# One projected map tile for two, the residual's copy in quarters, and a planner with two shared transfer queues

## The chip, the cores and the metric

The kernel runs on one core of one Trainium2 chip. Its time is the device time of one execution in microseconds (us); a kernel's figure is the median of several. A profiled execution gives the span from the first to the last instruction, and what each engine did in it. The engines are TensorE (PE in the profile, its weight loads PEld), VectorE (DVE), ScalarE (ACT), GpSimd (POOL) and SyncE (SP), which here only starts transfers.

## What is computed

Eight images of 256 channels and 32 x 32 pixels go through two layers.

```python
# layer 0: convolutional attention (8 heads of 32 channels)
q = einsum('bchw,oc->bohw', gn(x), q_w)
kv = einsum('bchw,oc->bohw', gn(x), kv_w)        # 256 key and 256 value channels
def pooled(t):                                    # four levels: 32, 16, 11 and 5 a side
    # average-pool each level, add its 3x3 depthwise convolution, join: 1,426 keys
ks, vs = layernorm(pooled(k_map)), layernorm(pooled(v_map))
attn = softmax(q k^T * scale);  out = attn v      # then a mix from a global token, projection
x = x + out
# layer 1: on tokens (1,024 an image)
t = t + attention(ln(t))                          # one head of 256
t = t + sum_e w[:, e] * (relu(bn(relu(bn(ln(t) W1[e])) W2[e])) Wo[e])   # 8 experts
```

## The kernel before

The program is written as one long order for each engine. `Flow` records every instruction (so nearly all have line 670, that of its `call`), and while the program is built it keeps an account: when each engine would be free, when each tile would be ready or read, what an operation costs (`cost`), and after an operation's end a lag until its result can be used (`note`). Work outside the main loop is written as generators ("threads") with a rank; a thread says what it needs next, and `step` resumes those that `runnable` lets go: filler for PE is let in while a credit lasts or while the account says that PE would stand otherwise. `finish` resumes threads until a condition holds, without regard to the credit. So the costs and lags of the account decide where every piece of filler is put in each engine's order; at run time the order is fixed and the engines wait for one another through semaphores.

The main loop of `attention` has 360 steps, 45 for each image b. The queries of one half of the heads (c) and one half of the pixels make a unit of 11 key chunks; the last, short chunk of all four units is done at once, as one more step of the first unit (`tail_scores`, the joint last keys). A step is: four score matmuls into `sc` (four PSUM banks, one buffer), the exponential by ACT into one of six `pt` tiles, and the value matmuls of the step before into `pv`. For the sums, every odd `pt` is added into the even one by an accumulating transfer started by POOL, and VectorE adds the pairs (`sums`).

Beside these steps run, as threads: `prepare(b)` for the next image (load into `xi`, group statistics, pooling, then `maps`), `convolve` (the taps of the depthwise convolution on VectorE, `taps`), `value_tokens` and `key_tokens` (transposes and layer norm, which make `vt` and `kn`), `queries` and `fetch_queries`, `project`, and layer 1 (`layer1`, `outputs`, `norm`). What of layer 1 is not done by the loop's end runs beside the first part of `experts`, until the gates, which need all images, are there; until then the second expert layer is done plainly and put by in DRAM (`ahead`), after that both layers use seven products of quarter size.

The names that the change touches:
- `pmaps`, tags `p0` and `p1` of 128 x 1,426 floats: a projected map, of which there are four for an image (two of values, two of keys). `maps` writes it by ACT in three slices (columns 0, 512 and 1,024 on) beside the scaled `acc`; `taps` reads it: level 0 (eight taps over the first 1,024 columns), then the three small levels. `todo` counts maps begun, `read[0]` those whose level 0 was read, `done` those finished, `freed[0]` the pairs of `acc` set free. In `maps` the next map is begun when

```python
lambda: read[0] >= len(todo) - 1 and len(todo) < (3 + 2 * max(freed[0], 2) if freed[0] else 5)
```

  and its third slice when `len(done) >= len(todo) - 1`.
- `first_maps` makes image 0's maps, with two borrowed `pt` tiles and the two of `pmaps` to hold them.
- the residual: x[b] is copied to `t1[b]` in DRAM by SP when `prepare(b)` begins, and `project(b)` adds to it with transfers started by POOL (`t<-xr`). In the profile the copy is `t<-in_x_dram`, 1,024 KB, seven times; the last image has none. `layer1` loads `t1[b]` later.
- the lag of a transfer in `note`: 2.0 us and 0.0045 us a KB for SP, 1.5 us and 0.0078 us a KB for POOL, whatever else is on its way.

Of the kernel before, what the change touches and what calls it, by code (L numbers as in the profile page):

```python
# [16 lines left out]
P = 128  # L17
C = 256
HW = 1024
# [637 lines left out]
class Flow:  # L657
# [27 lines left out]
    def __init__(self, tc, kit):  # L685
        nc = tc.nc
        self.tc, self.kit = tc, kit
        self.now = dict.fromkeys(("PE", "DVE", "ACT", "POOL", "SP"), 0.0)
        self.last = {}
        self.ready, self.read, self.writer, self.reader, self.slots, self.open = {}, {}, {}, {}, {}, set()  # L690
        self.pe = self.Engine(self, "PE", nc.tensor)
        self.ve = self.Engine(self, "DVE", nc.vector)
        self.act = self.Engine(self, "ACT", nc.scalar)
        self.pool = self.Engine(self, "POOL", nc.gpsimd)
        self.sp = self.Engine(self, "SP", nc.sync)
        self.threads = []
        self.cut = {}
        self.also = {}
        self.tiled = None
        self.columns = False  # L700
        self.credit, self.port = [0.0, 0.0], 0.0

    def tile(self, pool, shape, tag, bufs=1):
# [60 lines left out]
    def note(self, engine, op, ins, args, kwargs):  # L764
        aps = [a for a in (*args, *kwargs.values()) if hasattr(a, "tensor") or hasattr(a, "space")]
        out = kwargs.get("out", args[0] if args else aps[0])
        srcs = [a for a in aps if a is not out]
        prev = self.last.get(engine)
        if prev is not None:
            self.tc.add_manual_dep(  # L770
                ins.ins,
                prev,
                mybir.DependencyInfo(mybir.DependencyClass.NoSync, mybir.DependencyReason.DATA),
                reason="program order",
            )
        self.last[engine] = ins.ins.name
        start = self.now[engine]
        names = [n for a in srcs for n in self.keys(a)]
        outs = self.keys(out)
        for n in (*names, *outs):  # L780
            if self.writer.get(n) != engine:
                start = max(start, self.ready.get(n, 0.0))
        for o in outs:
            if self.reader.get(o, engine) != engine:
                start = max(start, self.read.get(o, 0.0))
        cost = self.cost(engine, op, out, srcs)
        if engine == "PE":

            tiling = None if op == "transpose" else self.tiling(srcs)
            if tiling != self.tiled:  # L790
                cost += {None: 0.2, "rows": 0.2, "columns": 0.13, "both": 0.2}[tiling]
                self.tiled = tiling

        wide = [a for a in srcs if a.space != PSUM and a.free_size() > 4]
        if "dma" not in op and engine == "POOL" or engine == "DVE" and wide and (len(wide) > 1 or op in ("tensor_scalar", "tensor_copy")):
            start = max(start, self.port)
            self.port = start + cost
        self.now[engine] = end = start + cost
        lag = 0.15
        if "dma" in op:  # L800
            size = 4e-3 * out.shape[0] * out.free_size() if out.space != DRAM else 4e-3 * srcs[0].shape[0] * srcs[0].free_size()
            lag = 2.0 + 0.0045 * size if engine == "SP" else 1.5 + 0.0078 * size
        for n in {*outs, self.key(out)}:
            self.ready[n] = max(self.ready.get(n, 0.0), end + lag)
            self.writer[n] = "DMA" if "dma" in op else engine
        self.open.difference_update(names)
        for n in {*names, *map(self.key, srcs)}:
            self.read[n] = max(self.read.get(n, 0.0), end + lag)
            self.reader[n] = engine

    @staticmethod
    def key(a):
# [85 lines left out]
def attention(tc, kit, f, outer, ended, nb, consts, x, t1, t2, hn, bounds, vecs, q_t, kv_t, proj_t, gqk_t, wqk, wqkv, vecs1, w1_d, w1c, gate_d, wrc, vecs2, bnvec):  # L898
# [6 lines left out]
    with ExitStack() as ctx:  # L905
# [165 lines left out]
            f.pool.memset(t, 0.0)  # L1071
        made = [0]
        turn = [-1]
        todo, done, read, freed, key_parts, normalised = [], [], [2], [0], [0], [0]

        def pe(*tiles, tag=None):
            return "PE", tiles, tag
# [20 lines left out]
        def maps(xp):  # L1098

            for m in (2, 3, 0, 1):  # L1100
                c = m % 2
                yield until(
                    lambda: read[0] >= len(todo) - 1 and len(todo) < (3 + 2 * max(freed[0], 2) if freed[0] else 5)
                )
                p = pmaps[len(todo) % 2]
                acc = T(work, [P, NK], "acc", bufs=3)
                for s0, w in KEY_SLICES:
                    if s0 >= HW:
                        yield until(lambda: len(done) >= len(todo) - 1)
                    src = source(xp, s0, w)  # L1110
                    yield pe(src, tag="sm")
                    ps = small()
                    for k in range(2):
                        f.pe.matmul(
                            ps[:, :w],
                            lhsT=kvw[:, k, m * P : (m + 1) * P],
                            rhs=src[:, k, :],
                            start=k == 0,
                            stop=k == 1,
                        )  # L1120
                    f.act.activation(p[:, s0 : s0 + w], ps[:, :w], AF.Copy)
                    for s, n in enumerate(SIDES):
                        a, z = max(OFFS[s], s0), min(OFFS[s] + n * n, s0 + w)
                        if a < z:
                            f.act.activation(
                                acc[:, a:z],
                                ps[:, a - s0 : z - s0],
                                AF.Identity,
                                bias=db(c, s),
                                scale=mid[:, c * 4 + s : c * 4 + s + 1],  # L1130
                            )
                todo.append((c, p, acc))
# [4 lines left out]
            return dy, dx, max(0, -dy), n - max(0, dy), max(0, -dx), n - max(0, dx)  # L1137


        pmaps = [T(work, [P, NK], f"p{i}") for i in range(2)]  # L1140
        for t in pmaps:
            f.split(t, 512, HW)
        first, large, whole, pooled, asked = {}, [], [], [], []

        def first_diagonals():
# [11 lines left out]
        def first_maps(xp):  # L1157


            for m in range(4):  # L1160
                if m < 2:
                    p = T(work, [P, 4, 512], "pt", bufs=6).rearrange("p j q -> p (j q)")
                    acc = T(l1, [P, NK], "v") if m else T(work, [P, NK], "kn", bufs=3)
                else:
                    p = pmaps[m - 2]
                    acc = T(work, [P, NK], "acc", bufs=3)
                for t in (p, acc):
                    if t is not p or m < 2:
                        f.split(t, 512, HW)
                first[m] = p, acc  # L1170
            for m, s0 in [(m, s0) for g in (0, 2) for s0 in (0, 512) for m in (g, g + 1)] + [(m, HW) for m in range(4)]:
# [70 lines left out]
        def first_taps():  # L1242
            for m in (2, 3):
                yield until(lambda: "maps" in large)
                yield from taps(m - 2, 0, *first[m])
                large.append(("values", m))
                read[0] += 1
            yield until(lambda: whole)
            for m in (2, 3, 0, 1):
                for s in range(1, 4):  # L1250
                    yield from taps(m % 2, s, *first[m])
                whole.append(m)
            done.extend(first[m][1] for m in (2, 3, 0, 1))
# [109 lines left out]
        def prepare(b):  # L1363
# [1 line left out]
            if b:  # L1365
                yield until(lambda: len(asked) == 4)
            xi = xs.pop(b) if b in xs else load_x(b)
            if b < nb - 1:
                f.sp.dma_start(t1[b], x[b].rearrange("(k p) n -> p k n", p=P))
            st = T(work, [P, 2, 2, 6], "st")  # L1370
            mv = T(work, [P, 2, 2], "mv")
            for k in range(2):
# [518 lines left out]
        for i in range(len(steps) + 1):  # L1891
            if i < len(steps):
                b, c, half, kc = steps[i]
                sl = slice(half * 512, half * 512 + 512)
                if kc % 4 == 0:
                    f.finish(lambda: key_parts[0] > 3 * b + kc // 4)
                if (half, kc) == (0, 0):
                    f.finish(lambda: (b, c) in qs and (b or (c, 0) in asked))
                    turn[0] = 2 * b + c
                    atts[b, c] = T(work, [P, HW], "att", bufs=2)  # L1900
                if i == 4:
                    f.finish(lambda: {0, 1}.issubset(whole))
                if b == 0 and kc == 0:
                    f.finish(lambda: (c, half) in asked)
                if kc == NKC - 1:
                    f.finish(lambda: key_parts[0] > 3 * b + 2 and (b, 1) in qs and (b or len(asked) == 4))
                    tail_scores(b)
                else:
                    pts[i] = scores(b, c, sl, kc)
                f.step()  # L1910
# [709 lines left out]
```

## Time and profile before

| | us |
|---|---|
| median of 3 runs | 3294.26 (3291.0 to 3302.8) |
| the profiled execution | 3300.42 |
| its span | 3298.6 |
| first and last exponential of the main loop | 82.7, 1877.7 |

Mean granted TensorE clock: 0.978. Transfers moved 388 MB, a mean of 118 GB/s: 179.85 MB in the queue that POOL starts (28.1% of 16 engines' span) and 202.59 MB in that of SP (18.0%).

A row of busy times gives for each engine the us in which it was busy, the share of the span, and the instructions. In the rows of stretches the columns are: from and to, length, then busy us (and instructions) of PE, PEld, DVE, ACT, POOL, then the clock, the share of the 16 DMA engines, and GB/s. A row of waits reads: who waited for whom, us in total, times, longest. A row of the timeline: start, us, engine, line, operation, out<-in, shapes, count, and in brackets the idle time of that engine just before and what ended it. Buffer numbers are left out of names, so `p` is a map here and also a probability tile of layer 1, and `t<-in_x_dram` is `t1[b]`.

### The profile page before, as it was taken

What the parts mean: (1) busy time and instruction counts of PE and PEld (TensorE: products, weight loads), DVE (VectorE), ACT (ScalarE), POOL (GpSimd) and SP (SyncE); (2) the same over time, 40 slices, a digit from 0 to 9 for tenths busy, and PEclk for the clock granted to TensorE, in tenths of its full rate; (3) what the DMA queues carried; (4) which work ended last, traced back from release to release, by engine and by line L of the source; (5) the groups of instructions that cost most, each with busy time, mean ns of one, the idle gap of its engine ahead of it and who ended that gap; (6) DMA issues with size and microseconds to landing.
All of it is one profiled execution on the core that took longest, in us unless ns stands there. A gap on an engine that the chain in (4) does not pass through costs nothing.

```text
span 3298.6 us, 55657 instructions
## 1 busy us (share of the span) xinstructions
PE 3093.2 (94%) x22264; PEld 1793.6 (54%) x22264; DVE 2466.9 (75%) x4060; ACT 1692.0 (51%) x2298; POOL 1174.7 (36%) x1269
## 2 busy tenths in 40 slices
PE   8787899989989979999999989999999999999998
PEld 4322234324334323343433447776888888888887
DVE  5787898888887878979754544444888888887776
ACT  4466667656666657566656423334333333344443
POOL 2212314122141141232121120002856555577776
PEclk9799999989999999999999999999999999999999
DMA  2358666665575565656576662214444344300000
GB/s 75 78 117 183 135 149 126 129 153 105 125 172 104 135 152 95 152 122 123 126 165 122 144 229 74 77 63 161 141 141 142 139 163 163 122 20 33 20 13 21
DMA packets 118524, 388.06 MB, mean 118 GB/s; under 512 B 14560, under 2 KB 40488, under 8 KB 95024
## 3 DMA queue, kind: packets, MB, share of 16 engines
q0 software_dynamic: 28608, 179.85, 28.1%
q1 hardware_dynamic: 86288, 202.59, 18.0%
q8 instruction: 177, 2.90, 0.4%
q10 hardware_dynamic: 3360, 1.97, 0.2%
q14 instruction: 91, 0.75, 0.1%
HBM read 125.03 MB, written 93.89 MB: 66 GB/s over the span
## 4 chain that ended last, share of the span: by engine, by line
PE 46%; DVE 4%; DMA 1%; ACT 1%; issue 1%; POOL 1%; SPq 0%; DVEq 0%; ACTq 0%; POOLq 0%
PE bank L670 21%; PE y L670 10%; PE sm L670 9%; PE sc L670 3%; PE pv L670 2%; PE sx L670 2%; DVE h L670 1%; DVE u L670 1%; DVE c L670 1%; ACT pt L670 1%; DVE t L670 0%; DMA pt<-pt 0%; DMA t<-t 0%; POOL t L670 0%; ACT h L670 0%
## 5 line engine op out<-in xcount | busy, mean ns | idle before, releaser
L670 ACT ACTIVATE pt<-sc 128x2048 f32<-128x2048 f32 x352 | 660.8, 1877 | 291.4 <-PE sc L670 226.4
L670 DVE SCALAR_TENSOR_TENSOR acc<-p,vec,acc 128x961 f32<-128x961 f32 (+3 forms) x960 | 565.0, 597 | 32.5 <-ACT acc L670 6.2
L670 PE MATMUL sc<-q,kn 32*128 32x512 f32 (+1 forms) x3072 | 425.4, 659 | 107.7 <-ACT pt L670 105.0
L670 DVE TENSOR_TENSOR pt<-pt,pt 128x1024 f32<-128x1024 f32 x320 | 391.1, 1267 | 125.3 <-DMA pt<-pt 92.7
L670 PE MATMUL pv<-pt,vt 128*32 128x512 f32 x2816 | 387.0, 622 | 0.0
L670 ACT ACTIVATE p1c<-bank 128x256 f32<-128x256 f32 x222 | 85.0, 383 | 562.5 <-PE bank L670 544.9
L670 ACT ACTIVATE h<-h,bnvec 128x512 f32<-128x512 f32 x444 | 335.7, 805 | 66.0 <-DVE h L670 58.2
L670 POOL TENSOR_TENSOR rstd<-rstd,mhalf 128x4 f32<-128x4 f32 (+2 forms) x88 | 107.0, 1216 | 734.6 <-DVE rstd L670 699.5
L670 POOL DMA_DIRECT2D pt<-pt x160 | 147.2, 920 | 565.7 <-ACT pt L670 399.2
L670 DVE TENSOR_TENSOR h<-p1c,bank 128x512 f32<-128x512 f32 x222 | 151.4, 682 | 217.2 <-PE bank L670 213.8
L670 PEld LDWEIGHTS sc<-q,kn 32*128 32x128 f32 (+1 forms) x3072 | 114.6, 180 | 303.2 <-ACT pt L670 198.3
L670 DVE TENSOR_TENSOR h<-u,bank 128x256 f32<-128x256 f32 (+1 forms) x444 | 226.1, 550 | 7.6
L670 POOL TENSOR_TENSOR tm<-h,tm 128x256 f32<-128x256 f32 x194 | 220.4, 1136 | 15.2
L670 PE MATMUL bank<-h,w2e 128*128 128x256 f32 (+1 forms) x636 | 215.6, 468 | 6.0 <-ACT h L670 3.4
L670 PEld LDWEIGHTS pv<-pt,vt 128*32 128x32 f32 x2816 | 56.1, 109 | 277.8 <-issue 264.8
L670 PE MATMUL sm<-p,v 128*32 128x256 f32 (+1 forms) x2328 | 200.2, 382 | 1.9 <-ACT sm L670 1.9
L670 DVE TENSOR_TENSOR h<-h,gate 128x1024 f32<-128x1024 f32 x128 | 196.0, 1531 | 0.5 <-ACT h L670 0.5
L670 POOL TENSOR_TENSOR tm<-h 128x512 f32<-128x512 f32 x97 | 129.8, 1338 | 181.4 <-ACT h L670 178.1
L670 PE MATMUL bank<-t,s1e 128*128 128x256 f32 x750 | 185.4, 383 | 5.5 <-DVE h L670 5.4
L670 PE MATMUL y<-t,s3e 128*128 128x256 f32 x768 | 187.0, 379 | 1.8 <-POOL t L670 1.8
L670 PE MATMUL sm<-y,t 128*32 128x256 f32 (+1 forms) x1872 | 178.7, 379 | 0.6 <-DVE st L670 0.6
L670 POOL TENSOR_TENSOR t<-h 128x512 f32<-128x512 f32 x100 | 129.7, 1297 | 131.8 <-DVE h L670 91.2
(317 smaller groups left out, 5506.9 us busy)
## 6 DMA issues: line engine op xcount, KB each, us to landing
pt<-pt POOLq DMA_DIRECT2D x160, 1024.0 KB, 7.9
h<-h SPq DMA_DIRECT2D x166, 512.0 KB
xi<-in_x_dram SPq DMA_DIRECT2D x16, 512.0 KB
t<-t SPq DMA_DIRECT2D x8, 1024.0 KB
res<-t SPq DMA_DIRECT2D x32, 256.0 KB
t<-res SPq DMA_DIRECT2D x32, 256.0 KB
hn<-res SPq DMA_DIRECT2D x32, 256.0 KB
hn<-hn SPq DMA_DIRECT2D x16, 512.0 KB
```

The source lines that it names most:

```text
L670: ins = fn(*args, **kwargs)
```

## The change

- `first_maps`, `maps`: one tile `pmap` (tag `p`) in the place of two. In image 0 the fourth map borrows an `acc` tile. A map is begun when level 0 of the map before has been read in the order (`read[0] >= len(todo)`, `read[0]` now begins at 4 and `first_taps` doesn't count), and its third slice when all its taps have been put in; the bound with `freed` becomes `3 + 2 * freed[0]`.
- `prepare`: the copy is taken out. In the main loop, at the seventh chunk (`kc == NKC // 2`) of every unit of image b, one quarter of it (128 channels by 512 pixels, 256 KB) is started by SP.
- `note`: the lag of a transfer comes from `transfer`, which keeps the work left in two queues (POOL's and all others), each at half speed while both have work; 5.5 us a MB for POOL's and for DRAM to DRAM, 3.1 us a MB otherwise, and 1.7 us on top.

```diff
--- before.py
+++ after.py
@@ -698,6 +698,7 @@
         self.also = {}
         self.tiled = None
         self.columns = False
+        self.left, self.served = [0.0, 0.0], 0.0
         self.credit, self.port = [0.0, 0.0], 0.0
 
     def tile(self, pool, shape, tag, bufs=1):
@@ -798,8 +799,9 @@
         self.now[engine] = end = start + cost
         lag = 0.15
         if "dma" in op:
+            both = out.space == DRAM and srcs[0].space == DRAM
             size = 4e-3 * out.shape[0] * out.free_size() if out.space != DRAM else 4e-3 * srcs[0].shape[0] * srcs[0].free_size()
-            lag = 2.0 + 0.0045 * size if engine == "SP" else 1.5 + 0.0078 * size
+            lag = self.transfer(engine, end, size * (0.0054 if engine == "POOL" or both else 0.003))
         for n in {*outs, self.key(out)}:
             self.ready[n] = max(self.ready.get(n, 0.0), end + lag)
             self.writer[n] = "DMA" if "dma" in op else engine
@@ -807,6 +809,19 @@
         for n in {*names, *map(self.key, srcs)}:
             self.read[n] = max(self.read.get(n, 0.0), end + lag)
             self.reader[n] = engine
+
+    def transfer(self, queue, at, work):
+
+        span = max(0.0, at - self.served)
+        self.served = max(self.served, at)
+        mine, other = queue == "POOL", queue != "POOL"
+        left = self.left
+        both = 2 * min(left)
+        done = min(span, both) / 2
+        for i in range(2):
+            left[i] = max(0.0, left[i] - done - max(0.0, span - both))
+        left[mine] += work
+        return 1.7 + left[mine] + min(left[mine], left[other]) + self.served - at
 
     @staticmethod
     def key(a):
@@ -1071,7 +1086,7 @@
             f.pool.memset(t, 0.0)
         made = [0]
         turn = [-1]
-        todo, done, read, freed, key_parts, normalised = [], [], [2], [0], [0], [0]
+        todo, done, read, freed, key_parts, normalised = [], [], [4], [0], [0], [0]
 
         def pe(*tiles, tag=None):
             return "PE", tiles, tag
@@ -1099,14 +1114,12 @@
 
             for m in (2, 3, 0, 1):
                 c = m % 2
-                yield until(
-                    lambda: read[0] >= len(todo) - 1 and len(todo) < (3 + 2 * max(freed[0], 2) if freed[0] else 5)
-                )
-                p = pmaps[len(todo) % 2]
+                yield until(lambda: read[0] >= len(todo) and len(todo) < 3 + 2 * freed[0])
+                p = pmap
                 acc = T(work, [P, NK], "acc", bufs=3)
                 for s0, w in KEY_SLICES:
                     if s0 >= HW:
-                        yield until(lambda: len(done) >= len(todo) - 1)
+                        yield until(lambda: len(done) >= len(todo))
                     src = source(xp, s0, w)
                     yield pe(src, tag="sm")
                     ps = small()
@@ -1137,9 +1150,8 @@
             return dy, dx, max(0, -dy), n - max(0, dy), max(0, -dx), n - max(0, dx)
 
 
-        pmaps = [T(work, [P, NK], f"p{i}") for i in range(2)]
-        for t in pmaps:
-            f.split(t, 512, HW)
+        pmap = T(work, [P, NK], "p")
+        f.split(pmap, 512, HW)
         first, large, whole, pooled, asked = {}, [], [], [], []
 
         def first_diagonals():
@@ -1162,10 +1174,10 @@
                     p = T(work, [P, 4, 512], "pt", bufs=6).rearrange("p j q -> p (j q)")
                     acc = T(l1, [P, NK], "v") if m else T(work, [P, NK], "kn", bufs=3)
                 else:
-                    p = pmaps[m - 2]
+                    p = T(work, [P, NK], "acc", bufs=3) if m == 3 else pmap
                     acc = T(work, [P, NK], "acc", bufs=3)
                 for t in (p, acc):
-                    if t is not p or m < 2:
+                    if t is not pmap:
                         f.split(t, 512, HW)
                 first[m] = p, acc
             for m, s0 in [(m, s0) for g in (0, 2) for s0 in (0, 512) for m in (g, g + 1)] + [(m, HW) for m in range(4)]:
@@ -1244,7 +1256,6 @@
                 yield until(lambda: "maps" in large)
                 yield from taps(m - 2, 0, *first[m])
                 large.append(("values", m))
-                read[0] += 1
             yield until(lambda: whole)
             for m in (2, 3, 0, 1):
                 for s in range(1, 4):
@@ -1365,8 +1376,6 @@
             if b:
                 yield until(lambda: len(asked) == 4)
             xi = xs.pop(b) if b in xs else load_x(b)
-            if b < nb - 1:
-                f.sp.dma_start(t1[b], x[b].rearrange("(k p) n -> p k n", p=P))
             st = T(work, [P, 2, 2, 6], "st")
             mv = T(work, [P, 2, 2], "mv")
             for k in range(2):
@@ -1898,6 +1907,8 @@
                     f.finish(lambda: (b, c) in qs and (b or (c, 0) in asked))
                     turn[0] = 2 * b + c
                     atts[b, c] = T(work, [P, HW], "att", bufs=2)
+                if kc == NKC // 2 and b < nb - 1:
+                    f.sp.dma_start(t1[b][:, c, sl], x[b, c * P : (c + 1) * P, sl])
                 if i == 4:
                     f.finish(lambda: {0, 1}.issubset(whole))
                 if b == 0 and kc == 0:
```

## The prediction

> **What bounds the kernel now.** I read first the page's busy times, then the stretches of the span, the waits, and the timeline around the longest idle times of TensorE.
>
> Busy times, and three stretches: batch 5 of the attention, the last batch, and the expert stage without layer 1.
>
> ```profile
> PE 3093.2 (94%) x22264; PEld 1793.6 (54%) x22264; DVE 2466.9 (75%) x4060; ACT 1692.0 (51%) x2298; POOL 1174.7 (36%) x1269
> ```
>
> ```profile
> 1221.00:1473.00 252.00, 241.47 (x2348) 97.40 (x2344) 213.46 (x377) 168.36 (x223) 70.66 (x85) 0.98 0.56 121
> ...
> 1689.00:1880.00 191.00, 184.72 (x2072) 68.25 (x2072) 98.97 (x125) 111.80 (x105) 34.94 (x40) 0.99 0.68 139
> ...
> 2270.00:3298.00 1028.00, 1004.72 (x4577) 869.20 (x4575) 807.18 (x1136) 374.68 (x616) 668.72 (x655) 0.99 0.28 98
> ```
>
> After a start-up of 82 us TensorE (first pair of columns) is busy 95 to 98% of a stretch, so work moved from one stretch to another costs nothing by itself. Only two things can change the time: how much PE work there is, and how long PE is idle. VectorE comes next, at 213 of 252 us.
>
> The attention loop has 360 steps (8 batches of 45): four score matmuls into `sc`, which fills four banks and has one buffer, the exponential that empties it, the value matmuls, and whatever filler the planner puts in. From the start times of the 360 exponentials (82.7 to 1875.9 us) and the columns of filler between two score tiles in the program's PE order, I get the period of a step: 3.14 us is the floor (61 steps have no filler; their median is 3.14), and with filler it is about 2.0 us + 1.72 ns a column (median 3.83 us at 1,067 columns, 7.67 at 3,443). So an empty step wastes 1.14 us of PE. Summed over the intervals that form gives 1684 us; measured are 1793. The other 109 are waits, 28 of them in one step of batch 0 where VectorE does the first small levels.
>
> What ends the waits inside the loop:
>
> ```profile
> PE sc L670 <- ACT pt L670: 105.0, 88, 4.7
> ...
> ACT pt L670 <- DMA pt<-pt: 35.5, 12, 5.9
> ```
>
> The exponential waits for a `pt` buffer that an accumulating DMA has not left. The worst place, on ACT, SP and PE (start, duration, idle before):
>
> ```profile
> 686.30 1.88 ACT L670 ACTIVATE pt<-sc 128x2048 f32<-128x2048 f32 x1 [1.26 <-PE sc L670]
> 694.03 1.88 ACT L670 ACTIVATE pt<-sc 128x2048 f32<-128x2048 f32 x1 [5.86 <-DMA pt<-pt]
> 700.29 1.88 ACT L670 ACTIVATE pt<-sc 128x2048 f32<-128x2048 f32 x1 [4.38 <-DMA pt<-pt]
> ```
>
> ```profile
> 680.62 0.88 SPq L670 DMA_DIRECT2D xi<-in_x_dram  x2
> 681.55 0.68 SPq L670 DMA_DIRECT2D t<-in_x_dram  x1
> ```
>
> ```profile
> 688.23 1.14 PE L670 MATMUL sc<-q,kn 32*128 32x512 f32 x8 [1.00 <-ACT pt L670]
> ...
> 695.96 2.09 PE L670 MATMUL sc<-q,kn 32*128 32x512 f32 x8 [4.74 <-ACT pt L670]
> ```
>
> The reader is to see a burst: two loads of 512 KB and the residual's copy of 1 MB go out together, and accumulates issued beside them land after 13.6 and 13.9 us (median 7.7). PE stands 4.74 us and then runs at half speed (2.09 for 1.14). The excess over the step formula near the bursts of four batches is 4.6+3.1+2.6, 4.3+1.2+1.4, 3.7 and 2.1: 23 us in all.
>
> **What the Trainium skill says.** "DMA: Bandwidth & Descriptors", section "Issuing engines are not separate DMA queues": transfers started by SP and by GpSimd run on the same 16 DMA engines and interleave. The trace agrees: 13.6 us beside the burst for a usual 7.7. "TensorE: Matmul & The Clock Gate", Part 1: after an idle window of some 3.4 us the array runs at half clock until it has been busy again. The trace agrees: 2.09 us for 1.14 after 4.74 idle; after 1.00 idle nothing. No page bears on the planner.
>
> **The change part by part.** I compare the two programs' instruction order on each engine. The new account of transfers moves fillers everywhere, so the parts are told apart by what they touch.
>
> *Filler moved, by the account.* Filler in the attention loop goes from 512,412 to 550,300 columns (+37,888), after it from 806,530 to 767,106 (-39,424): three more of layer 1's 32 query tiles are finished inside the loop (nine were left after it, now six). The formula gives 1741.7 us for the loop, +57.5, which is 7.6 less than 37,888 x 1.72 ns = 65.2: steps with no filler fall from 61 to 56. After the loop, 39,424 columns less at 1.72 ns are -67.8. **Sum -10.3 us.** Of this 2.6 is real work: second expert layers done plainly fall from 31 to 25 (four matmuls of 512 columns, 248 in the row, become seven of 256: 256 columns less each). Those six add 24 VectorE and 18 GpSimd instructions (0.42 to 0.68 and about 1.2 us) in a stretch where these engines are busy 807 and 669 of 1028 us beside PE; and 36 transfers of 512 KB fewer (166 to 130). I cost these at nothing.
>
> *The copy in quarters.* Seven copies of 1 MB become 28 of 256 KB, one in each unit's seventh step, SP issue 0.3 to 0.7 us each. They are queued on SP ahead of loads of `t`, `res` and `q` that are needed tens of us later; the project step's accumulates, which need the last quarter, come about ten steps after it. Gone: at most the 23 us; the two `xi` loads stay, near the end of a batch, whose last step now has much filler. I take 14. New: one quarter can cost from 0 to 4.6/4 = 1.15 us, where the step is near its floor, which 91 of 359 are: 28 x 0.25 x 1.15 = 8. **Net -6 us** (bounds -23 and +32). At the start, copies at 1.6 and 37.7 us go; PE there waits for VectorE behind `xi`, issued before the copy: 0.
>
> *One map tile.* The next map's copy by ACT must wait for VectorE's taps on the previous one; behind it in ACT's queue stands the exponential, and PE behind that. Today six maps have a copy two or three steps after those taps in the order, and the trace shows one wait for them, 0.83 us. Now 21 maps are so placed, first and third slice, mostly three to five steps behind, seven slices two or less. From 0 to 42 x 0.83 = 35; I take some 0.4 us for each of the seven: **+3**.
>
> *Keys just in time.* The next batch's last map now comes in steps 30 to 36 of a batch (before, 17 to 28), so its first keys are transposed in step 43 or 44 and the others after it has begun, at all seven boundaries; before, batches 6 and 7 had all theirs by step 44 and most by 37. The last step's filler rises to 10,500 and 10,200 columns for batches 5 and 6 (before 4,600 and 2,300): the planner waits there and gives layer 1's work to PE meanwhile. Price: batch 5's start, the same case, shows 3.0+1.2+3.8 = 8.0 us over the formula, batch 1's 2.4, the other three 0: 10.4 now. Seven boundaries at 0 to 8.0 are -10 to +46; I take 3 each: **+11**.
>
> *Other waits for `pt` buffers* (0.7 to 4.6 us each) may be better or worse placed by the new account: -9 to +9, taken as 0.
>
> Sum: -10.3 - 6 + 3 + 11 = **-2 us**. The profiled execution took 3300.4 (span 3298.6 and 1.8 around it), 6.2 above the median; so 3298 against it, and 3292 against the median of 3294.3.
>
> **Rivals.** *Faster: every wait is filled.* The planner meets the key chain with layer 1's filler and the quarters vanish in fuller steps: boundaries 0 (-10.4 for +11) and no 8 for quarters: 29 us less, 3263. For it: fewer empty steps, fewer tile-mode switches on PE (198 for 212). Against: the 109 us of waits that are there although the planner meant none.
> *Slower: the keys are late.* If each boundary costs what batch 5's did, 8.0 for my 3, it is +35: 3327. It decides from 5.7 us a boundary on. For it: seven for five boundaries, VectorE at 85% of batch 5, and a chain over five engines. Against: four of five such boundaries cost 2.4 or less.
> *The copies don't matter*, the burst being the `xi` loads': 14 us less gain, 3306.
>
> **How the numbers follow.** Within 0.5% (16.5 us, about what a measurement can tell from none): 0.43, the sum and the last rival. Slower by more: 0.32, late keys, or quarters and tile waits nearer their upper bounds. Faster by more: 0.25. The range runs from just below the fast case to just above the slow one, 3258 to 3335; the likeliest case's own is 3278 to 3308.
>
> **What would show it.** Right: the loop ends some 45 to 60 us later (1877.7 before) and the part after it is shorter by about as much; no exponential waits 4 us or more for `pt<-pt` at steps 30 to 36; waits of `p<-sm` for `acc` stay below 10 us; PE stands a few us in steps 44 to 4 of each batch. Wrong: PE idle over 6 us at most batch starts (slow), ACT waiting for `acc` by tens of us, or the loop's end moving without the rest giving it back.

## The result and the profile after

The changed kernel takes 3313.0 us (median of 4 runs, 3310.6 to 3318.0) against 3294.7 (four runs, one more than above): a ratio of 1.0054, interval 1.0032 to 1.0076. It is slower by 18 us where the prediction had 2 us faster. The profiled execution took 3311.8 (span 3309.9), so the two profiles differ by 11.3 us of span; that is what the traces can explain.

The busy times of the page after, and the three stretches that answer to those of before (batch 5, the last batch, the last 1028 us of the span):

```profile
PE 3088.9 (93%) x22732; PEld 1795.6 (54%) x22732; DVE 2452.7 (74%) x4066; ACT 1693.4 (51%) x2304; POOL 1207.6 (36%) x1305
```

```profile
1273.00:1518.00 245.00, 229.39 (x2377) 94.17 (x2374) 195.95 (x331) 151.16 (x190) 61.78 (x68) 0.98 0.61 132
1770.00:1964.00 194.00, 185.27 (x1940) 73.65 (x1938) 99.78 (x143) 118.96 (x123) 35.67 (x42) 1.00 0.66 136
2281.00:3309.00 1028.00, 1008.12 (x4643) 879.62 (x4641) 810.43 (x1141) 385.28 (x633) 695.84 (x672) 1.00 0.22 77
```

PE, VectorE and ACT do nearly the same work as before. PE is busy in 229 of 245 us of batch 5 (94%; before, 241 of 252, 96%), and as before in the last stretch. Over the whole span PE's busy time fell by 4.3 us and the time in which it stands rose by 15.6: that is the difference of 11.3.

| us | before | after |
|---|---|---|
| first exponential | 82.7 | 81.4 |
| last exponential's end | 1877.7 | 1964.2 |
| from there to the end of the span | 1420.9 | 1345.8 |
| step formula, summed over the loop | 1684.2 | 1741.7 |
| measured periods less formula | 108.9 | 139.3 |
| of it: seven boundaries (step 43 of a batch to step 7 of the next) | 14.1 | 45.1 |
| of it: batch 0, steps 0 to 42 | 52.2 | 53.5 |
| of it: all other steps | 42.6 | 40.6 |
| PE idle, whole span | 198.1 | 213.7 |
| time at half clock, whole span | 143.8 | 160.3 |
| of it while PE was busy | 110.8 | 109.9 |

So 57.5 us of filler came into the loop, the part after it became 75.1 shorter, and 31 us were lost at the boundaries: 57.5 + 31.0 + 1.3 - 2.0 - 75.1 - 1.3 = 11.4. Two of the seven boundaries carry it: 25.3 (before 2.6) at the start of batch 1 and 14.5 (before 3.8) at that of batch 6. The clock did not add to it: the record has 16.5 us more at half clock, but they lie where PE stood anyway.

The waits after:

```profile
PE sc L670 <- ACT pt L670: 96.2, 91, 5.3
...
ACT p L670 <- DVE acc L670: 51.4, 24, 5.7
...
ACT pt L670 <- DMA pt<-pt: 18.2, 9, 4.6
...
DVE st L670 <- DMA xi<-in_x_dram: 16.1, 6, 4.2
```

The exponential's wait for a `pt` buffer is halved (35.5 before). Two waits are new: ACT's map copies wait for VectorE's taps on the one tile (0.8 us before), and VectorE's statistics wait for the next image's load (none before).

The timeline at the end of batch 0, on SP, VectorE, ACT and PE:

```profile
309.01 2.47 SPq L670 DMA_DIRECT2D xi<-in_x_dram  x2
```

```profile
319.88 1.29 DVE L670 BATCH_NORM_STATS2 st<-xi 128x6 f32<-128x512 f32 x2 [1.86 <-DMA xi<-in_x_dram]
321.20 0.21 DVE L670 BATCH_NORM_AGGREGATE mv<-st 128x2 f32<-128x12 f32 x1
321.33 0.11 DVE L670 SCALAR_TENSOR_TENSOR tshift<-tmean,rstd 128x4 f32<-128x4 f32 x1
325.48 1.29 DVE L670 BATCH_NORM_STATS2 st<-xi 128x6 f32<-128x512 f32 x2 [4.04 <-DMA xi<-in_x_dram]
```

```profile
321.53 2.07 ACT L670 ACTIVATE kt<-kt,tshift,rstd 128x256 f32<-128x256 f32 x4 [5.40 <-DVE tshift L670]
328.64 0.60 ACT L670 ACTIVATE kn<-sm 128x512 f32<-128x512 f32 x1 [5.03 <-PE sm L670]
```

```profile
327.06 0.59 PE L670 MATMUL sx<-mv,con 128*128 128x2 f32 x2 [11.83 <-DVE mv L670]
327.51 1.95 PE L670 MATMUL sm<-con,kt 128*128 128x128 f32 x8
329.38 2.09 PE L670 MATMUL sc<-q,kn 32*128 32x512 f32 x8
331.41 1.94 PE L670 MATMUL pv<-pt,vt 128*32 128x512 f32 x8
```

Read it from PE backwards. Two tiny matmuls for the statistics of image 2 stand in PE's order ahead of the transposes of image 1's first keys; they wait for `mv`, and PE stands 11.83 us. `mv` waits on VectorE for the second load of `xi`, issued at 309 and used at 325.5. The key's own shift, `tshift`, stands on VectorE behind the first half of these statistics. Then PE runs at half clock: 2.09 us for 1.14, 1.94 for 1.06. Of the 12 places in the loop where PE stands over 3 us (64 us; before, 8 places and 32 us), this is the largest.

The other costly boundary, at the end of batch 5, has the same root on VectorE, and the chain goes on through ACT:

```profile
1492.50 1.29 DVE L670 BATCH_NORM_STATS2 st<-xi 128x6 f32<-128x512 f32 x2 [4.22 <-DMA xi<-in_x_dram]
1498.07 1.29 DVE L670 BATCH_NORM_STATS2 st<-xi 128x6 f32<-128x512 f32 x2 [4.04 <-DMA xi<-in_x_dram]
```

```profile
1501.26 0.39 ACT L670 ACTIVATE sm<-rec 128x256 f32<-128x256 f32 x1 [10.90 <-DVE rec L670]
```

```profile
1501.82 1.11 PE L670 MATMUL sm<-con,acc 128*128 128x128 f32 x4 [6.60 <-ACT sm L670]
```

The reciprocal `rec` stands on VectorE behind the statistics of image 7, ACT waits 10.90 us for it, and PE 6.60 us for ACT. Of VectorE's 16.1 us of waits for `xi`, 14.2 lie at these two boundaries.

### The profile page after: what moved, and what is told of

It reads as the page before. It is cut to its first block, busy times and chain, and to the rows that moved or that the text cites. A ratio compares the mean times of both kernels' runs of the same rounds, so it can differ in the third digit from the quotient of the medians.

```text
span 3309.9 us, 56632 instructions
## 1 busy us (share of the span) xinstructions
PE 3088.9 (93%) x22732; PEld 1795.6 (54%) x22732; DVE 2452.7 (74%) x4066; ACT 1693.4 (51%) x2304; POOL 1207.6 (36%) x1305
## 4 chain that ended last, share of the span: by engine, by line
PE 69%; DVE 12%; DMA 6%; ACT 5%; issue 5%; POOL 2%; SPq 0%; DVEq 0%; ACTq 0%; POOLq 0%
PE bank L670 21%; PE sm L670 17%; PE y L670 10%; PE sc L670 8%; PE sx L670 7%; PE pv L670 6%; DVE acc L670 3%; ACT pt L670 3%; DMA pt<-pt 3%; DVE pt L670 2%; DVE rec L670 1%; DVE h L670 1%; DMA xi<-in_x_dram 1%; DMA pt<-ptail 1%; DVE u L670 1%
## 5 line engine op out<-in xcount | busy, mean ns | idle before, releaser
L670 DVE SCALAR_TENSOR_TENSOR acc<-p,vec,acc 128x225 f32<-128x225 f32 (+7 forms) x928 | 530.0, 577 | 33.5 <-ACT acc L670 8.8
L670 ACT ACTIVATE h<-h,bnvec 128x512 f32<-128x512 f32 x456 | 344.9, 805 | 64.4 <-DVE h L670 55.4
L670 POOL TENSOR_TENSOR tm<-h,tm 128x256 f32<-128x256 f32 x206 | 238.3, 1157 | 16.1
L670 DVE TENSOR_TENSOR h<-u,bank 128x256 f32<-128x256 f32 x456 | 232.3, 550 | 7.8
L670 PE MATMUL bank<-h,w2e 128*128 128x256 f32 (+1 forms) x612 | 199.5, 455 | 1.9 <-DVE h L670 1.9
L670 ACT ACTIVATE p<-sm 128x512 f32<-128x512 f32 (+1 forms) x156 | 91.3, 585 | 166.6 <-PE sm L670 126.8
L670 POOL TENSOR_TENSOR t<-h 128x512 f32<-128x512 f32 x106 | 137.1, 1294 | 106.7 <-DVE h L670 84.0
```

What stands on the lines that cost most here:

```text
L670: ins = fn(*args, **kwargs)
```

## The experiments

The change has three separable parts: T, the one tile with its three conditions in `maps`; Q, the copy in quarters; A, the account. In the tables "boundaries" is the sum of the seven boundaries over the step formula, and "lost" is PE's idle time with half of the half-clock time in which PE was busy; both are of the profiled execution. In all 20 profiles the span less "lost" is 3035 to 3047 us, while "lost" runs from 191 to 295: it is the column that moves the time. Each ratio is to runs of before taken beside the kernel's own, whose medians are 3294.0 to 3298.2.

### The parts, alone and in pairs

Each kernel is the one before with the named hunks of the diff, or the one after without them.

```diff
 e1 = before + T      e2 = before + Q      e3 = before + A
 e4 = after - T       e5 = after - Q       e6 = after - A
```

> The kernel before with one map tile for two, and nothing else; the copy stays whole and the account old. Theory 1 (the single tile spreads the next image's four maps over the batch, so its queries, the load of xi after it and the first keys fall together at the batch's end, and ACT waits for the taps): 15 to 30 us slower than before, ACT waits of p for acc over 30 us, PE standing several us at some batch starts. Theory 2 (the new account's short lag for SP's transfers is what puts VectorE's statistics of xi in front of the key chain): within 6 us of before. The step formula (2.0 us + 1.72 ns a column, floor 3.14) gives +7 us from the order alone, as 73 steps have no filler for 61.

> The kernel before with the residual's copy in quarters, and nothing else; filler on PE stays as it was. If the 1 MB copy made the waits for pt buffers at steps 30 to 36: 8 to 20 us faster than before and no such wait over 3 us. If the two xi loads made them: within 5 us of before. If the quarters cost where the steps are at their floor: up to 10 us slower.

> The kernel before with the new account of transfers, and nothing else. Theory 1: within 6 us of before (the formula gives -1). Theory 2: 10 to 20 us slower, with VectorE waiting for xi by more than before.

> The changed kernel with two map tiles again: quarters and account, not the tile. Theory 1: 15 to 30 us faster than the changed kernel, so 0 to 15 us faster than before. Theory 2: as slow as the changed kernel, 12 to 20 us over before.

> One map tile and the new account; the residual's copy whole. Alone they gave -0.54% and -0.66%, quarters with the account -1.64%, all three +0.54%. If the loss of all three is an interaction of tile and account (both put the next image's work at the batch's end): 15 us or more slower than before. If it takes the quarters (which make SP's other transfers look early in the account): within 10 us of before or faster.

> One map tile and quarters, with the old account, whose order on PE is that of the tile alone. If quarters do nothing by themselves, as without the tile: within 5 us of the tile alone (3277). If they collide with the next image's loads at the batch's end: 8 us or more slower than that.

| | us | ratio to before [95%] | boundaries | lost |
|---|---|---|---|---|
| before | 3294.7 | 1 | 14.1 | 254 |
| e1, T | 3276.7 | 0.9946 [0.9932, 0.9960] | 20.0 | 233 |
| e2, Q | 3295.7 | 1.0006 [0.9996, 1.0016] | 13.2 | 246 |
| e3, A | 3272.8 | 0.9934 [0.9919, 0.9949] | 18.1 | 234 |
| e4, Q and A | 3236.1 | 0.9836 [0.9821, 0.9850] | 4.4 | 191 |
| e5, T and A | 3285.3 | 0.9963 [0.9951, 0.9976] | 30.3 | 250 |
| e6, T and Q | 3278.7 | 0.9940 [0.9919, 0.9961] | 19.0 | 232 |
| after, all three | 3313.0 | 1.0054 [1.0032, 1.0076] | 45.1 | 269 |

No part is slow alone; two of them measure half a per cent faster. The three together lose. The tile is faster by 0.5% on the kernel before, and slower by 2.2% on the kernel with Q and A. The parts of this planned order do not add up. (Whether half a per cent belongs to a part or to the order that it happened to give is asked further down.)

Of the expectations, "theory 1" (the tile alone is slow) and "theory 2" (the account alone is slow) both fell: e1 and e3 came out 17 and 21 us faster. e4 came out on theory 1's side, by far more than it allowed. e2 and e6 came out as if the quarters did nothing by themselves. e5 met the case in which the loss takes the quarters: with them the kernel is at 1.0054, with the copy whole at 0.9963.

e2 also tells that the copy did not make the burst's waits. At the burst of batch 2, on ACT and SP:

```profile
689.20 1.88 ACT L670 ACTIVATE pt<-sc 128x2048 f32<-128x2048 f32 x1 [6.52 <-DMA pt<-pt]
694.81 1.88 ACT L670 ACTIVATE pt<-sc 128x2048 f32<-128x2048 f32 x1 [3.73 <-DMA pt<-pt]
```

```profile
675.56 0.90 SPq L670 DMA_DIRECT2D xi<-in_x_dram  x2
676.51 1.31 SPq L670 DMA_DIRECT2D t<-in_x_dram  x2
```

The copy of 1 MB is down to two quarters here, and the exponential waits as before (5.86 and 4.38); over the whole kernel its waits for `pt` are 35.9 us for 35.5. Halving the copy bought nothing. The loads of `xi` are still there, and so are the accumulates; which of them makes the waits was not tried.

### What in the tile costs: the buffer, the pace, or the statistics

```diff
 e7: after, in prepare, ahead of the statistics
+            if b > 1:
+                yield until(lambda: key_parts[0] > 3 * (b - 1))
 e8: after, in maps (both tiles made as before)
-                p = pmap
+                p = pmaps[len(todo) % 2]
```

> The changed kernel, but the group statistics of an image (VectorE, which waits for the load of xi) are put into the order only when the first keys of the image before have been made. If VectorE standing for xi in front of the key chain is the main loss: steps 44 of batches 0 and 5 lose their 10 to 13 us over the formula each, and the kernel is 15 to 30 us faster than the changed one. If ACT's waits of p for acc are the main loss: within 8 us of the changed one.

> The changed kernel with two map tiles, used in turn, but begun only when the one tile would have been free: the pace of the change without its buffer. If ACT's wait for the taps (51 us) is the loss: that wait is below 8 us and the kernel is 25 us or more faster than the changed one. If the later preparation is the loss, it stays within 10 us of the changed one, whatever becomes of ACT's wait.

e7: 3343.3 us, 1.0132 [1.0104, 1.0160]. VectorE's wait for `xi` is gone, and PE's 11.83 us at the end of batch 0 with it (4.93 there now, for `kt`); the formula's own sum rises by 11 us and the boundaries stay at 48.7. Delaying the statistics took that wait away and moved the time elsewhere (the last maps come later still, at step 36.7 on average for 33.1), so the expectation that VectorE's wait was the main loss fell; so did its rival, ACT's waits, since the kernel is 30 us slower than the changed one.

e8: 3302.8 us, 1.0017 [1.0010, 1.0024]. With a second buffer ACT no longer waits for the taps, and 10 of the 77 us between after and e4 come back, at the edge of what the later preparation was given. Most of what the tile does is done by the conditions under which a map is begun, not by the buffer. The 76 us between the profiles of e4 and after lie about so: boundaries 41, batch 0 up to step 42 13, other steps 17, and 6 in the filler that moved (formula +39.5, the part after the loop -33.5).

### The three conditions one by one, and a way round one

```diff
 e9: e4, only the third slice's condition
-                        yield until(lambda: len(done) >= len(todo) - 1)
+                        yield until(lambda: len(done) >= len(todo))
 e10: e4, only the bound: len(todo) < 3 + 2 * freed[0]
 e11: e4, only level 0: read[0] >= len(todo), read[0] from 4
 e12: after, the third slice with two places in a longer tile
-        pmap = T(work, [P, NK], "p")
+        pmap = T(work, [P, 2 * NK - HW], "p")
-                        yield until(lambda: len(done) >= len(todo))
+                        yield until(lambda: len(done) >= len(todo) - 1)
 ... (and the slice is written and read at its place in turn)
```

> Base: the kernel after with two map tiles (3236 us). One of the three conditions of the one-tile version is put in alone: a map's third slice is let in only when all taps of the map before have been put in the order. All three together, with two tiles, gave 3303. Theory 'third slice': this condition ties every map to the small levels of the one before, so it carries most of the 67 us: 3280 to 3305, and the loop's residual over the step formula rises from 68 to about 100. By its order it has 21,500 more filler columns in the loop and 74 empty steps for 61 (step formula and columns after the loop together +11 us). Rival 'read' or 'freed': 3236 to 3252, the order's +11 at most.

> Base: the kernel after with two map tiles (3236 us). Only the bound 3 + 2 * freed is put in alone, which holds image 1's first maps back until image 0's keys are in and all later ones as before. Theory 'freed': the losses lie in batches 0 and 1, where image 1 is prepared, so this bound carries them: 3270 to 3300, with a residual of batches 0 and 1 of 70 to 80 us for 50. Theory 'third slice': no more than its order says, 3236 to 3250 (step formula and columns together +4 us).

> Base: the kernel after with two map tiles (3236 us). Only the condition on level 0 is put in alone: a map is begun when level 0 of the map before, not of the one before that, has been read in the order. Its order differs little from the base (768 columns fewer in the loop, the same 61 empty steps; step formula and columns together -2 us). Theory 'third slice' or 'freed': 3228 to 3245. Rival 'read': beginning a map late is what makes the keys late, 3265 to 3300.

> The kernel after (3313 us), its map tile lengthened by 402 columns: the first 1,024 columns are shared as there, the third slice has two places used in turn and the old bound (one map earlier). Theory 'third slice': this bound makes the loss, so most of it goes: 3255 to 3285, between the runs with the freed bound and the level-0 bound alone (3257 and 3279) and little above. Rival 'the shared level 0': 3300 to 3320. Its order has 529,000 columns of filler in the loop, with 61 empty steps.

| | us | ratio to before [95%] | last map, mean step | boundaries | lost |
|---|---|---|---|---|---|
| e4, none | 3236.1 | 0.9836 [0.9821, 0.9850] | 22.6 | 4.4 | 191 |
| e10, bound | 3257.2 | 0.9880 [0.9864, 0.9897] | 24.6 | 5.0 | 225 |
| e11, level 0 | 3278.5 | 0.9946 [0.9930, 0.9963] | 26.4 | 6.8 | 238 |
| e9, third slice | 3311.9 | 1.0055 [1.0038, 1.0072] | 35.9 | 34.3 | 269 |
| e8, all three, two tiles | 3302.8 | 1.0017 [1.0010, 1.0024] | 34.4 | 25.3 | 255 |
| after | 3313.0 | 1.0054 [1.0032, 1.0076] | 33.1 | 45.1 | 269 |
| e12, after with two third slices | 3274.5 | 0.9937 [0.9913, 0.9962] | 29.0 | 30.9 | 233 |

"Last map" is the step, of the batch before, in which the third slice of an image's last map stands in PE's order (mean of seven images). The third slice's condition alone, with both buffers there, is as slow as all of the change (76 of 77 us, 7 more than its theory allowed); giving the slice a second place in the kernel after takes 1.2% away, as its theory had it. e10 lies between the two theories, and e11 came out as the rival 'read' had it, not as its theory. The three single costs (21, 42 and 76 us) do not add up to that of all three (67), and the next part shows that the two smaller ones are no larger than what a shift without meaning can do to e4.

### How far an order moves by itself

The last six runs ask whether such differences mean anything. One constant of the account is moved by 0.1 us, and nothing else; such a shift alone moves up to 17,700 columns of filler into or out of the loop. (In e16 to e18 the same question is put to a third order of after and of e4, and a second of e6.)

```diff
 e13, e16: after; e14, e17: e4 (1.8 in e13 and e14, 1.6 in e16 and e17)
-        return 1.7 + left[mine] + ...
+        return 1.8 + left[mine] + ...
 e15: before; e18: e6
-            lag = 2.0 + 0.0045 * size if engine == "SP" else 1.5 + 0.0078 * size
+            lag = 2.1 + 0.0045 * size if engine == "SP" else 1.6 + 0.0078 * size
```

> The kernel after (3313 us), with 1.8 us for 1.7 in the lag that the account gives a transfer; nothing else. Theory 'fixed price': within 10 us of it, 3303 to 3323. Theory 'scatter of orders': it moves by 10 to 50 us, and in the direction of the middle of the orders seen (3236 to 3343, mean about 3285): 3270 to 3305. By its order, 9,700 columns fewer in the loop and 10,000 more after it.

> The kernel after with two map tiles (3236 us), with 1.8 us for 1.7 in the lag of a transfer; nothing else. Theory 'fixed price': 3226 to 3246. Theory 'scatter of orders': the fastest order so far was partly luck, 3250 to 3285.

> The kernel before (3294 us), with 0.1 us more in the lags of both kinds of transfer (2.1 and 1.6 us); nothing else. Theory 'fixed price': 3284 to 3304. Theory 'scatter of orders': 10 to 40 us away, on either side; its order has 78 empty steps for 61 and step formula and columns together +15 us, so rather slower: 3300 to 3330.

> The kernel after, with 1.6 us for 1.7 in the lag that the account gives a transfer. Its last map's third slice still comes late (steps 28 to 36 of the batch before, mean 33). Theory 'late maps cost': stays above 3290, 3295 to 3315. Rival 'chance': anywhere from 3240 to 3320, and as likely below 3280 as above.

> The kernel after with two map tiles, with 1.6 us for 1.7 in the lag of a transfer. Last third slice in steps 15 to 31, mean 23. Theory 'late maps cost': below 3280, 3240 to 3275. Rival 'chance': anywhere from 3240 to 3320.

> The kernel before with one map tile and with quarters (3279 us), with 0.1 us more in the old account's lags (2.1 and 1.6 us). Last third slice in steps 29 to 39, mean 34. Theory 'late maps cost under either account, and e1, e5 and e6 were orders that happened to be good': 3290 to 3325 (its order has 81 empty steps for 73, step formula and columns together +8 us). Theory 'only under the new account': 3265 to 3295.

| | ratio to before, order by order | last map | boundaries | PE gaps over 3 us in the loop |
|---|---|---|---|---|
| after, e13, e16 | 1.0054, 1.0030, 1.0045 | 33.1, 34.9, 32.6 | 45, 55, 28 | 64, 59, 58 us |
| e4, e14, e17 (two tiles) | 0.9836, 0.9899, 0.9954 | 22.6, 26.1, 22.6 | 4, 14, 15 | 19, 24, 31 us |
| before, e15 | 1, 0.9925 | 21.4, 26.3 | 14, 14 | 32, 27 us |
| e6, e18 (T and Q) | 0.9940, 0.9963 | 34.6, 34.7 | 19, 33 | 29, 41 us |

(Intervals: e13 [1.0016, 1.0045], e14 [0.9872, 0.9925], e15 [0.9900, 0.9950], e16 [1.0031, 1.0059], e17 [0.9936, 0.9972], e18 [0.9952, 0.9975].)

A shift without meaning moves the time by up to 1.2% (e4 to e17) and that of the kernel before by 0.75%. e13 came out as "fixed price" had it, e16 as "late maps cost", e18 as "only under the new account"; e14 and e15 came out beyond what "fixed price" allowed, e15 on the faster side, where its order spoke for slower; e17, at 3282.7 us, is above what "late maps cost" gave it. So the half per cent of e1, e3 and e6 (which has e1's order on PE) isn't shown to belong to the part that was changed, nor the 21 and 42 us of e10 and e11. Yet the groups keep apart: with Q and A, three orders with one tile are at 1.0030 to 1.0054 and three with two tiles at 0.9836 to 0.9954, 1.5% between their means, and the boundaries and the gaps of PE divide in the same way. The third slice's condition divides all twelve kernels that have Q and A: the six with it (after, e7, e8, e9, e13, e16) are at 1.0017 to 1.0132, the six without it (e4, e10, e11, e12, e14, e17) at 0.9836 to 0.9954. That it is this condition that costs, beside Q and A, is shown; the size of the price, which each order shifts, is not. Under the old account the tile has no such price: e1, e6 and e18, whose last maps come as late, are all 0.4 to 0.6% below before. And under the new account without the quarters (e5, last maps at 34.3) it is small: 0.3% above e3. What the quarters do to it stays open.

A likely reason why late maps cost under one account and not under the other is seen at the same place in e1, on VectorE:

```profile
304.20 0.16 DVE L670 SCALAR_TENSOR_TENSOR tshift<-tmean,rstd 128x4 f32<-128x4 f32 x1 [1.22 <-POOL rstd L670]
...
310.75 1.29 DVE L670 BATCH_NORM_STATS2 st<-xi 128x6 f32<-128x512 f32 x2 [2.49 <-DMA xi<-in_x_dram]
...
315.73 1.29 DVE L670 BATCH_NORM_STATS2 st<-xi 128x6 f32<-128x512 f32 x2 [3.45 <-DMA xi<-in_x_dram]
```

The loads are as late there (17 us before the boundary, 22 in after, 49 in before), and VectorE waits for them too; but a first `tshift` of image 1's keys stands ahead of the statistics, and PE has no gap over 3 us there. With tile and account the gap at step 44 of batch 0 is there in after, e5, e8, e12, e13 and e16 (7.7 to 11.8 us), and in none of the runs without the tile's conditions. It is a part of the loss only: e5 and e12 have it in full and are 0.4 and 0.6% below before, and e7 lost it and gained nothing. The costly start of batch 6 comes in after and e7 alone, and in e7 without VectorE's wait for `xi`. That the account's lag for `xi` is what puts the statistics too early is the likely reason, and was not tried by itself.

## Why the prediction was wrong, step by step

- *Filler moved, by the account*: the mechanism held. The loop took the 57.5 us of the formula; the part after it gave back 75.1 for 67.8. The step is 7 us better than it was costed, by luck: PE stands 9.9 us less after the loop (28.1 for 38.0), which the prediction put at nothing.
- *Keys just in time*: this step failed. It was mis-sized, +11 for a measured +31 (14.1 to 45.1; the prediction counted 10.4 for these 14.1). Each boundary was priced by batch 5's in the trace before, 3 us taken and 8 at most. Two boundaries took 25.3 and 14.5 and the other five 5.4 together. What was missed is that the next-but-one image's load follows a late last map (issued 22 us before batch 1 for 49), so that at these two boundaries its statistics come into the same steps as the keys: their instructions stood ahead on PE and VectorE, and both engines stood for data that nobody needed yet. The order compared before the run showed the late maps; it was not followed one thread further, to `xi`. How much of the 31 us the late `xi` makes stays open, since in e7 the time came back elsewhere.
- *The copy in quarters*, -6: alone it is 0 (e2), as the rival "the copies don't matter" had it. The kernel's waits for `pt` did fall by 17 us in the loop, and none of 4 us was left at steps 30 to 36, but they fell as far in e1, without quarters (15.6 us), and the residual outside boundaries and batch 0 fell by 2 only.
- *One map tile*, +3: ACT's wait is 51 us, over the upper bound of 35. It was priced by a single wait of 0.83 us; measured are 24 of 2.1. It seems to cost little: with a second buffer e8 gained 10 us, and a shift without meaning moved after by up to 8 (e13).
- *Other waits and the start*, 0: right in sum only, by luck; batch 0 up to step 42 moved by 1.3. Step 3 of it rose from 28.1 to 37.8 us over the formula: PE stands 8.9 us for `rec`, where before it made the first map of image 1, which the new bound holds back (e10, with the bound alone, shows it too). The other steps gave back 8.4.
- The signs: ACT waiting for `acc` by tens of us was named as a sign of the slow case, and it came; PE standing over 6 us came at two boundaries, not at most of them. The loop's end moved 86 us for 45 to 60, because the 31 came on top.
- *Half clock* had no term of its own, and needed none: with PE busy it was 110.8 us before and 109.9 after.

The slow rival had the right place, late keys at the boundaries; its even distribution over them was not what came. The runs also show that a shift of the account by 0.1 us, which no step-by-step sum can price, moves the time by 0.1 to 1.2%; the whole change is worth 0.5%, so the likeliest case was given more chance than such a sum can carry.

## What to carry to other kernels

Where a planner writes the order, price a change of its conditions by what the order does with the next transfer and the next image, not by the waits of the buffer that is shared: here a second buffer gave back 10 of 77 us, and the pace that the one buffer forced made most of the rest. Before a difference below one per cent is put down to a part, shift a constant without meaning and see how far the order moves; then compare groups of orders. Two map tiles with the new account and the quarters were the best version, 0.5 to 1.6% below before in three orders (3236 us in the first); another order of before itself (e15) is 0.75% below it.

## What was not expected of the hardware

Two loads of `xi`, 512 KB each, issued between 309.0 and 311.5, let VectorE start on them at 319.9 and 325.5, 10.9 us after the first issue began and 14.0 us after the second ended; the new account gives such a load 1.7 us and 1.6 us of work beyond what is queued. How much of the difference was other transfers in the queues was not measured. And the 11.83 us gap on PE cost more than its length: after it the score matmuls took 2.09 us for 1.14 and the value matmuls 1.94 for 1.06. Yet time at half clock is not all loss: 33 of 143.8 us of it before, and 50 of 160.3 after, passed while PE stood.
